# Local attention with q and k kept feature major: rotation halves swapped by DMA, norms applied by GpSimd

## The chip, the cores and the metric

The program runs on one core of one Trainium2 chip. The core has four compute engines that run their own instruction queues in order: TensorE (PE in the profile, its weight loads PEld), VectorE (DVE), ScalarE (ACT) and GpSimd (POOL). SyncE (SP) issues most DMAs; POOL issues some. The metric is device time in microseconds (us) of one execution; less is better.

## The reference, cut to what matters

The whole kernel is four blocks of attention and feed-forward. The change lies in the second stage, `L0_ffn`: two layers of rotary local attention with a gated feed-forward behind it, on 2 sequences of 1024 tokens, which the kernel cuts into 4 blocks of 512 tokens.

```python
qkv = shift_token(x) @ wqkv              # 128 -> 3 * 512
q = l2norm(q) * qs                       # per head of 64: q / sqrt(sum q^2)
k = l2norm(k) * ksc
q = q*cos*scale + rotate_half(q)*sin*scale
k = k*cos/scale + rotate_half(k)*sin/scale
o = local_attention(q, k, v)             # 8 heads, windows of 64 see themselves and the one before
```

`rotate_half` puts the second half of a head's 64 features, negated, before the first. The norm of a token's head is one number, so it can be multiplied in before or after the rotation.

## The kernel before, in words

Class `F0` is this stage. A *unit* is one block of 512 tokens in one layer; there are 8 units (u = 0 to 7; the second layer begins at u = 4). A unit has three parts.

`qkv` (L1593) makes the operands. It transposes x, and then, for each chunk `c` of 128 tokens, multiplies it by the weights three times (q, k, v; `mm3` is three matmuls, L313 to L315, for accuracy), with the tokens on the partitions. For q and k the result is copied by ACT (L1632), squared by ACT (L1635), multiplied on DVE by the sine table in two halves with the halves crossed (L1639) and by the cosine table (L1641), and the squares are summed per head on DVE (L1642). For q the sum of the two products is left to the transposes, which accumulate in PSUM (L1655), and ACT copies the transposed q out (L1656). For k POOL adds the products (L1649). After the four chunks the reciprocal roots are made on DVE (`rsqrt`, L344 to L355); k is multiplied by them on DVE (L1669), transposed and copied out (L1676). The norms of q are left to `score`, which takes them as a scalar.

`scores`/`score` (L1692, L1705, L1707), `turn` (L1717), `shifted` (two POOL DMAs, L1725 and L1726) and `values` (L1736) are the attention, in 8 items per unit, one for each head. `post` (L1746 on) is the output projection, layer norm and feed-forward.

The order of the work is written out by generators. `run` (L1860) goes through the items; `qkv` of unit u+1 (list `A`) is stepped while the items of unit u are issued, `na` = 5 steps for each item, and `posts` (list `B`) `nbt` = 4 steps. A `yield` ends a step. The items of unit u+1 are not issued before its `qkv` is through. The framework then orders each engine's queue by this priority and by when it thinks operands are ready, and sets all the waits. A tile with a `tag` and `bufs=n` has n buffers, and the next user of a buffer waits until all readers of the last are done. `qT`, `kT` and `v` have one buffer for even and one for odd units. `qkv(0)` runs beside the last part of the stage before (its `yield from wait()` takes turns there). `weights_qkv(1)` loads and splits the second layer's weights behind `qkv(3)`; `weights_post(1)` follows `post(3)`.

Of the kernel before, what the change touches and what calls it, by code (L numbers as in the profile page):

```python
# [16 lines left out]
P = 128  # L17
# [1468 lines left out]
def f0_constants():  # L1486
# [13 lines left out]
    rot = out.astype(np.float32).reshape(4, 4, P, 64).transpose(2, 0, 1, 3)  # L1500
# [5 lines left out]
    return {"c_rot": np.ascontiguousarray(rot), "c_band": band, "c_sel8": heads(8)}  # L1506


class F0:
# [3 lines left out]
    wait_rn, wait_h, wait_h7, wait_ta, na, nbt, nta, la, np, ns, npt, pk = 8, 5, 8, 2, 5, 4, 2, 2, 4, 1, 3, 0  # L1513
    banks = dict(s=2, t=2, o=1, b=3)

    def __init__(self, k):
        self.k, self.nc = k, k.nc
        self.w, self.S, self.den = {}, {}, {}
# [12 lines left out]
    def weights_qkv(self, l):  # L1531

        k, nc, d, pool, w = self.k, self.nc, self.k.d, self.more, self.w
        w["qkvh"], w["qkvl"], fill = k.split_w(pool, d["f0_wqkv"][l], 1536, f"wqkv{l}", tag="wqkv")

        tab = k.load(pool, d["c_rot"], [P, 4, 4, 64], f"tab{l}", tag="tab")
        s = [k.bcast(pool, d[nm][l], 64, f"{nm}{l}", tag=nm) for nm in ("f0_qs", "f0_ks")]
        yield from fill
        for j in range(2):
            nc.gpsimd.tensor_tensor(tab[:, 2 * j], tab[:, 2 * j], s[j][:, None, :].to_broadcast([P, 4, 64]), ALU.mult)  # L1540
            for a, b in ((0, 32), (32, 0)):
                nc.gpsimd.tensor_tensor(tab[:, 2 * j + 1, :, a:a + 32], tab[:, 2 * j + 1, :, a:a + 32],
                                        s[j][:, None, b:b + 32].to_broadcast([P, 4, 32]), ALU.mult)
            yield
        w["tab"] = tab

    def weights_post(self, l):
# [15 lines left out]
        raw = k.load(self.more, d["f0_w1"][l], [P, 682], f"w1raw{l}", tag="wraw")  # L1563
# [21 lines left out]
    def operands(self):  # L1585
        k, nc, pool = self.k, self.nc, self.more
        self.xs = [pool.tile([P, T + 1], F32R, name=f"f0x{n}") for n in "hl"]
        for t in self.xs:
            nc.gpsimd.memset(t[64:P, 0:1].bitcast(F32), 0.0)

        self.x0 = [k.dr.tile([P, 4, P], F32, tag=f"f0x0{b}", name=f"f0x0{b}", bufs=1) for b in range(NB)]

    def qkv(self, u, X, tag="t"):  # L1593
# [22 lines left out]
        kr = pool.tile([P, 4, 512], F32, tag="kr", name=f"kr{u}", bufs=1)  # L1616
        ss = pool.tile([P, 2, 4, 8], F32, tag="ss", name=f"ss{u}", bufs=2)
        for _ in range(2):
            yield
        for c in range(4):  # L1620
            cs = slice(c * P, (c + 1) * P)
            for s in range(3):
                yield from wait()
                ps = k.bank("b")
                ws = slice(512 * s, 512 * s + 512)
                k.mm3(ps, xh[:, cs], xl[:, cs], w["qkvh"][:, ws], w["qkvl"][:, ws])
                if s == 2:
                    nc.scalar.copy(v[:, c, :], ps)
                    yield
                    continue  # L1630
                x = kr[:, c, :] if s else pool.tile([P, 512], F32, tag="ta", name=f"ta{u}{c}", bufs=self.nta)
                nc.scalar.copy(x, ps)  # L1632
                yield
                sq = pool.tile([P, 512], F32, tag="sq", name=f"sq{u}{c}{s}", bufs=1)
                nc.scalar.activation(sq, x, AF.Square)  # L1635
                tb = pool.tile([P, 8, 64], F32, tag="tb", name=f"tb{u}{c}{s}", bufs=2)
                x3 = x.rearrange("p (h d) -> p h d", d=64)
                for a, b2 in ((0, 32), (32, 0)):
                    nc.vector.tensor_tensor(tb[:, :, a:a + 32], x3[:, :, b2:b2 + 32],  # L1639
                                            w["tab"][:, 2 * s + 1, c, None, a:a + 32].to_broadcast([P, 8, 32]), ALU.mult)  # L1640
                nc.vector.tensor_tensor(x3, x3, w["tab"][:, 2 * s, c, None, :].to_broadcast([P, 8, 64]), ALU.mult)  # L1641
                nc.vector.tensor_reduce(ss[:, s, c, :], sq.rearrange("p (h d) -> p h d", d=64), AX.X, ALU.add)  # L1642
# [765 lines left out]
```

## Time and profile before

| what | value |
|---|---|
| median of 3 runs (range) | 2244.88 us (2244.24 to 2246.5) |
| profiled execution, its span | 2239.62 us, 2237.9 us |
| PE, DVE, ACT, POOL busy in the span | 91%, 74%, 60%, 22% |
| first score matmul (L1692) of units 0 to 7 | 238.2, 280.7, 322.3, 373.9, 438.7, 482.4, 534.7, 596.4 us |
| last score matmul of unit 7 | 625.4 us |

A *period* is the time from one unit's first score matmul to the next one's. A busy time is the time in which at least one instruction of a group runs. "Releaser" is what ended the idle time before an instruction.

### The profile page before, as it was taken

Reading aid. Unit: us, or ns where it says so; the run is one execution under the profiler, and the core shown is the slowest. Engines: PE = TensorE matmul, PEld = TensorE weight load, DVE = VectorE, ACT = ScalarE, POOL = GpSimd, SP = SyncE. Lnnn points to the kernel's source line nnn. Section 1 sums busy time; section 2 is a strip of 40 time slices with the busy share of each in tenths; the row PEclk is TensorE's granted clock in tenths of the full one; section 3 lists DMA queues with packets and bytes.
Section 4 is the critical chain, followed back from the end, with each engine's and each line's share of the span. In section 5 each row is a group of like instructions: output and inputs, shape, how many; then the busy total and the mean of one; then the engine's idle time right before and its main releaser. Section 6 shows DMA issues by size and latency. Waiting matters only on the chain.

```text
span 2237.9 us, 43122 instructions
## 1 busy us (share of the span) xinstructions
PE 2025.4 (91%) x14400; PEld 1477.7 (66%) x14400; DVE 1664.1 (74%) x5592; ACT 1333.5 (60%) x2983; POOL 501.9 (22%) x706
## 2 busy tenths in 40 slices
PE   7999788888888999999999999998999999999897
PEld 4666566676665667676887665786666566666676
DVE  5778689888878677873777785544777877778787
ACT  3566787787734656665333666333777777767632
POOL 3222212111212532433000322531111111111220
PEclk9999999999978999999999999999999999999999
DMA  5321322021433454421021420604888878888400
GB/s 171 106 77 35 109 50 57 6 48 27 116 113 108 130 175 125 127 65 57 15 67 48 116 78 15 219 17 112 214 209 198 211 192 193 199 194 211 99 5 15
DMA packets 264918, 242.10 MB, mean 108 GB/s; under 512 B 106352, under 2 KB 190618, under 8 KB 263866
## 3 DMA queue, kind: packets, MB, share of 16 engines
q1 hardware_dynamic: 259146, 221.33, 37.2%
q0 software_dynamic: 5232, 17.50, 3.3%
q8 instruction: 115, 1.88, 0.3%
q14 instruction: 105, 0.86, 0.1%
q10 hardware_dynamic: 320, 0.52, 0.1%
HBM read 103.82 MB, written 74.32 MB: 80 GB/s over the span
## 4 chain that ended last, share of the span: by engine, by line
PE 59%; DVE 17%; ACT 10%; DMA 7%; issue 4%; POOL 2%; SPq 1%; ACTq 0%; POOLq 0%; DVEq 0%
PE t L219 5%; PE s L2129 4%; PE o L1393 3%; PE o L744 3%; PE s L695 3%; PE t L728 3%; PE o L1032 3%; PE b L313 3%; PE b L219 3%; PE o L2025 3%; DMA a3dpw<-p 2%; PE s L313 2%; PE b L315 2%; PE b L314 2%; PE s L315 2%
## 5 line engine op out<-in xcount | busy, mean ns | idle before, releaser
L985 DVE CUSTOM_DVE_ANT_0 junk<-w,a1mask 128x640 bf16<-128x640 f32 x256 | 203.1, 818 | 67.3 <-PE w L983 65.4
L219 PE MATMUL t<-ident,p 128*128 128x128 f32 x1280 | 201.9, 279 | 23.8 <-ACT p L1350 15.7
L772 ACT ACTIVATE Pt<-t 128x384 f32<-128x384 f32 (+1 forms) x384 | 179.5, 528 | 65.8 <-PE t L728 54.4
L219 PEld LDWEIGHTS t<-ident,p 128*128 128x128 f32 x1280 | 151.7, 142 | 81.0 <-ACT p L1350 39.0
L1363 ACT COPY PT<-t 128x512 f32<-128x512 f32 x256 | 149.9, 596 | 71.9 <-PE t L219 70.9
L1059 ACT ACTIVATE Pt<-t 128x512 f32<-128x512 f32 x256 | 149.1, 597 | 72.7 <-PE t L1058 44.5
L1350 ACT ACTIVATE p<-s,nb 128x512 f32<-128x512 f32 x256 | 178.6, 702 | 12.8 <-DVE nb L1349 8.4
L1349 DVE TENSOR_REDUCE nb<-s 128x1 f32<-128x512 f32 x256 | 175.0, 687 | 2.6
L1368 DVE CUSTOM_DVE_ANT_0 jk<-p,a3right 128x496 bf16<-128x496 f32 (+3 forms) x256 | 125.0, 488 | 29.2 <-ACT p L1350 17.8
L697 DVE CUSTOM_DVE_ANT_0 junk<-s,a0mask 128x128 bf16<-128x128 f32 (+3 forms) x256 | 114.2, 485 | 43.4 <-PE s L695 42.4
L697 DVE CUSTOM_DVE_ANT_0 junk<-s,a2mask 128x128 bf16<-128x128 f32 (+3 forms) x256 | 114.9, 484 | 28.3 <-PE s L695 27.9
L781 POOL TENSOR_SCALAR_AFFINE_SELECT Pt<-Pt 128x512 f32<-128x512 f32 x112 | 69.9, 636 | 249.0 <-ACT Pt L772 248.9
L1344 PE MATMUL s<-a3KT,a3QT 128*128 128x512 f32 x256 | 118.9, 465 | 7.3 <-DMA a3K<-L 4.1
L1347 DVE TENSOR_TENSOR s<-s,W 128x160 f32<-128x160 f32 (+1 forms) x256 | 81.1, 318 | 56.1 <-PE s L1345 55.2
L1393 PE MATMUL o<-PT,V 128*64 128x512 f32 x512 | 116.9, 599 | 0.5 <-ACT PT L1363 0.5
L1707 ACT ACTIVATE p<-sm,nb 128x128 f32<-128x128 f32 x256 | 100.6, 396 | 24.8 <-DVE nb L1705 24.3
L1345 PE MATMUL s<-a3K,a3Q 128*128 128x512 f32 x256 | 102.7, 401 | 0.1
L1705 DVE CUSTOM_DVE_ANT_0 sm<-s,band,rn 128x128 f32<-128x128 f32 x256 | 78.3, 344 | 26.5 <-PE s L1692 19.3
L1056 PE MATMUL t<-a1Q,a1K 128*128 128x512 f32 (+3 forms) x256 | 92.4, 366 | 6.2 <-ACT Pt L1059 3.6
L695 PE MATMUL s<-a0K,a0Q 128*128 128x256 f32 (+2 forms) x256 | 83.6, 387 | 14.0 <-DVE mx L697 6.8
L982 PE MATMUL w<-a1K,a1Q 128*128 128x256 f32 (+2 forms) x192 | 83.8, 437 | 9.3 <-DVE mx L985 8.3
L2012 ACT ACTIVATE sl<-s 128x512 f32<-128x512 f32 x64 | 38.0, 598 | 91.0 <-PE s L315 85.6
(494 smaller groups left out, 5812.7 us busy)
## 6 DMA issues: line engine op xcount, KB each, us to landing
W<-a3dsk SPq DMA_DIRECT2D x32, 640.0 KB
a1Q<-a1iq SPq DMA_DIRECT2D x32, 512.0 KB
a3dpw<-p SPq DMA_DIRECT2D x64, 160.0 KB
a3dpw<-p SPq DMA_DIRECT2D x64, 144.0 KB
a1K<-a1ik SPq DMA_DIRECT2D x64, 128.0 KB
a3Q<-a3dim SPq DMA_DIRECT2D x32, 256.0 KB
a3KT<-H POOLq DMA_DIRECT2D x64, 128.0 KB, 4.4
a3KT<-H SPq DMA_DIRECT2D x64, 128.0 KB
```

The lines of the kernel that those rows point to most:

```text
L219: return self.nc.tensor.matmul(out.bitcast(x.dtype), x, i[:n, :n], is_transpose=True, start=start, stop=stop)
L695: self.scored = nc.tensor.matmul(s[:, :nm], self.qof(0, t, i)[:, qc * P:(qc + 1) * P], Ks[:, i, :nm], start=True, stop=True).ins
L697: nc.vector.tensor_tensor_reduce(junk[:, :n], s[:, :n], k.mask[:, 512 - n:512], 1.0, NEG, ALU.add, ALU.max, mx[:, qc, i:i + 1])
L772: ready = nc.scalar.activation(Pt[:, i, z:], s[:, z:], AF.Exp, scale=sc).ins
L985: nc.vector.tensor_tensor_reduce(junk, s.rearrange("p a n -> p (a n)")[:, T - n:T + m], k.mask[:, T - n:T + m], 1.0, NEG, ALU.add, ALU.max ...
L1059: nc.scalar.activation(Pt[:, i, :T], s, AF.Exp, scale=sc)
L1344: nc.tensor.matmul(s, QT[:, e, qs], KT[:, e, :], start=True, stop=False)
L1349: nc.vector.tensor_reduce(nb, s, AX.X, ALU.min)
L1350: nc.scalar.activation(p[:, e, :], s, AF.Exp, bias=nb, scale=-1.0, accum_out=den[:, qc, 2 * un + e:2 * un + e + 1])
L1363: self.copied[t] = nc.scalar.copy(PT[e][:, :, qc * P:qc * P + P], tb.rearrange("p (c n) -> p c n", n=P)).ins
L1368: nc.vector.tensor_tensor_reduce(jk[:, :nn], p[:, e, x0:], w["right"][:, :nn], 1.0, 0.0, ALU.mult, ALU.add, at[:, e, qc, 31:32])
L1393: m = nc.tensor.matmul(o[64 * e:64 * e + 64, :], V[:, kc, h * 64:h * 64 + 64], PT[e][:, kc, :], start=(kc == 0), stop=False)
```

## The change

q and k are computed with the features on the partitions: the weights' 128 columns (two heads) are the stationary operand and the 512 tokens stream, so no transposes of q and k follow. For the rotation, a pair of such blocks (`x`, 128 x 2 x 512) is copied by four DMAs on SP into `y` with its groups of 32 partitions exchanged; DVE multiplies `x` by the cosine table into `qT` or `kT`, later `y` by the sine table, and POOL adds the two (`rotate`). The tables are now feature major (1 MB instead of 512 KB) and are scaled on POOL by a column that 12 small DMAs load. The squares (ACT, into the unit's still empty `v`) are summed over each head by a matmul with a 128 x 32 matrix of ones; ACT copies the sums out, POOL's DMAs write them to DRAM, read them back with 128 partitions, DVE makes the reciprocal roots, a POOL DMA writes these to DRAM, and eight POOL DMAs read them back, each row broadcast to 64 partitions. POOL multiplies `qT` and `kT` by them. `score` uses 1.0 instead of the norm. `na` is 6, the extra yields of unit 0 and after `rsqrt` are gone, and the raw `w1` of `weights_post` takes a buffer of the tag `x`, which has two.

```diff
-    wait_rn, wait_h, wait_h7, wait_ta, na, nbt, nta, la, np, ns, npt, pk = 8, 5, 8, 2, 5, 4, 2, 2, 4, 1, 3, 0
+    wait_h7, na, nbt, la, np, ns, npt = 8, 6, 4, 2, 4, 1, 3
...
-        for j in range(2):
-            nc.gpsimd.tensor_tensor(tab[:, 2 * j], tab[:, 2 * j], s[j][:, None, :].to_broadcast([P, 4, 64]), ALU.mult)
...
+        for j in range(4):
+            nc.gpsimd.tensor_scalar(tab[:, j], tab[:, j], sc[:, j:j + 1], None, ALU.mult)
...
-        raw = k.load(self.more, d["f0_w1"][l], [P, 682], f"w1raw{l}", tag="wraw")
+        raw = k.load(self.more, d["f0_w1"][l], [P, 682], f"w1raw{l}", tag="x", bufs=2)
...
+        for s in range(2):
+            dst = (qT, kT[:, :, 64:])[s]
+            for i in range(4):
                 yield from wait()
                 ps = k.bank("b")
+                ws = slice(512 * s + P * i, 512 * s + P * i + P)
+                k.mm3(ps, w["qkvh"][:, ws], w["qkvl"][:, ws], xh[:, 0:T], xl[:, 0:T])
+                if i % 2 == 0:
+                    x = pool.tile([P, 2, T], F32, tag="x", name=f"x{u}{s}{i}", bufs=2)
+                nc.scalar.copy(x[:, i % 2], ps)
+                if i % 2:
+                    y = pool.tile([P, 2, T], F32, tag="y", name=f"y{u}{s}{i}", bufs=2)
+                    for o in (0, 32, 64, 96):
+                        nc.sync.dma_start(y[o:o + 32], x[o ^ 32:(o ^ 32) + 32])
                 yield
+                nc.scalar.activation(v[:, i], x[:, i % 2], AF.Square)
+                nc.vector.tensor_tensor(dst[:, i], x[:, i % 2], w["tab"][:, 2 * s], ALU.mult)
                 yield
+                if i % 2:
+                    for e in range(2):
+                        self.swaps.append((y[:, e], w["tab"][:, 2 * s + 1], dst[:, i - 1 + e]))
+                if len(self.swaps) > 2:
+                    self.rotate()
             yield from wait()
+            ps = k.bank("b")
+            for i in range(4):
+                nc.tensor.matmul(ps[32 * i:32 * i + 32], self.half, v[:, i], start=True, stop=True)
+            yield
+            sr = pool.tile([P, 2, T], F32, tag="x", name=f"sr{u}{s}", bufs=2)
+            nc.scalar.copy(sr[:, 0], ps)
+            for r in range(2):
+                nc.gpsimd.dma_start(rows[8 * s:8 * s + 8].rearrange("(i r) n -> r i n", r=2)[r], sr.rearrange("(i r) a n -> r i a n", r=32)[r, :, 0, :])
+        ss = pool.tile([P, 2, T], F32, tag="x", name=f"ss{u}", bufs=2)[:, 0, 0:64]
+        flat = lambda d: d.rearrange("h (a n) -> (h a) n", n=64)
+        nc.gpsimd.dma_start(ss, flat(rows))
+        for c in range(4):
+            if self.swaps:
+                self.rotate()
...
+            k.mm3(ps, xh[:, cs], xl[:, cs], w["qkvh"][:, 1024:1536], w["qkvl"][:, 1024:1536])
+            nc.scalar.copy(v[:, c, :], ps)
+            yield
+        nc.vector.tensor_scalar(ss, ss, 1e-24, None, ALU.max)
+        y = yield from k.rsqrt(pool, ss, 64, 1)
+        back = k.dr.tile([16, T], F32, tag="f0rn", name=f"f0rn{u}", bufs=2)
+        nc.gpsimd.dma_start(flat(back), y)
+        rn = []
+        for i in range(5):
+            if i < 4:
+                rn.append(pool.tile([P, 2, T], F32, tag="x", name=f"rn{u}{i}", bufs=2))
+                for e in range(2):
+                    src = bass.AP(tensor=back.tensor, offset=back.offset + (8 * (i % 2) + 4 * (i // 2) + e) * T, ap=[[0, 64], [2 * T, 2], [1, T]])
+                    nc.gpsimd.dma_start(rn[i][64 * e:64 * e + 64], src)
+            if i:
+                for e in range(2):
+                    z = (qT, kT[:, :, 64:])[(i - 1) % 2][:, (i - 1) // 2 * 2 + e]
+                    nc.gpsimd.tensor_tensor(z, z, rn[i - 1][:, e], ALU.mult)
+            yield
+        self.S[u] = (qT, kT, v)
+
+    def rotate(self):
+
+        y, tab, dst = self.swaps.pop(0)
+        self.nc.vector.tensor_tensor(y, y, tab, ALU.mult)
+        self.nc.gpsimd.tensor_tensor(dst, dst, y, ALU.add)
```

## The prediction

> **What bounds the stage now.** I read the page first: PE is busy 91% of the whole span, but the change touches only the units between 238.2 and 596.4 us, so I read busy time by windows, one for each period of that stage.
>
> ```profile
> core 0: us, PE busy (x) PEld busy (x) DVE busy (x) ACT busy (x) POOL busy (x), PEclk, DMA share, GB/s
> 238.20:280.70 42.50, 33.95 (x375) 25.96 (x374) 36.20 (x142) 33.37 (x101) 10.97 (x15) 0.92 0.51 138
> 280.70:322.30 41.60, 33.60 (x413) 26.61 (x413) 35.60 (x136) 34.36 (x109) 7.69 (x8) 1.00 0.21 55
> 322.30:373.90 51.60, 45.06 (x462) 35.33 (x463) 45.98 (x152) 40.26 (x111) 12.01 (x15) 0.90 0.16 40
> 373.90:438.70 64.80, 53.82 (x491) 41.37 (x492) 53.04 (x180) 46.35 (x125) 10.25 (x10) 0.90 0.11 29
> 438.70:482.40 43.70, 38.76 (x439) 31.24 (x439) 39.16 (x139) 34.71 (x106) 7.71 (x8) 0.96 0.16 37
> 482.40:534.70 52.30, 44.19 (x475) 35.67 (x475) 45.57 (x165) 40.63 (x113) 7.75 (x8) 0.96 0.12 27
> 534.70:596.40 61.70, 50.02 (x480) 39.00 (x480) 53.75 (x167) 44.08 (x119) 13.64 (x12) 0.93 0.33 94
> ```
>
> The columns are the window, its length, and each engine's busy time. The seven periods sum to 358.2 us and DVE is busy 309.3 of them (86%); the period follows DVE's work (36 us of work in 42, 54 in 62). PE (84%) and ACT (76%) are close behind and POOL idles (20%). Next, the timeline at a unit's start:
>
> ```profile
> 320.90 0.58 ACT L1676 COPY kT<-t 128x512 f32<-128x512 f32 x1 [0.95 <-PE t L219]
> 322.13 0.69 DVE L1669 TENSOR_TENSOR kr<-kr,rn 128x512 f32<-128x512 f32 x1
> 322.28 0.70 PE L1692 MATMUL s<-kT,qT 64*64 64x128 f32 x8 [0.75 <-ACT p L1707]
> ```
>
> A unit's scores start about 1 us after its first kT copy (in every unit: kT at 279.8, 320.9, 372.8, 438.0, 479.6, 534.0, 595.7). So the chain through `qkv` ends last in each period, and DVE's throughput is what paces it.
>
> **DVE.** The groups of the stage, name, shape, count, busy time and mean ns:
>
> ```profile
> L1649 POOL TENSOR_TENSOR kr<-kr,tb 128x512 f32<-128x512 f32 x28 | 35.8, 1278 | 156.2 <-DVE kr L1641 121.4 <-DVE rs L351 8.4 <-DVE rs L344 6.5
> L1641 DVE TENSOR_TENSOR kr<-kr,tab 128x512 f32<-128x512 f32 x28 | 19.2, 684 | 2.0 <-ACT sq L1635 1.9
> ...
> L1639 DVE TENSOR_TENSOR tb<-kr,tab 128x256 f32<-128x256 f32 x56 | 21.7, 422 | 1.6 <-ACT kr L1632 1.4
> ```
>
> Removed per unit: 16 half products (0.42 to 0.49, 7.2 us), 8 products (5.5), 8 sums of squares at 0.678 (5.4), 4 norm products at 0.683 (2.7): 20.8. Added: 8 + 8 products of L1641's shape, 10.9. Net -9.9 us a unit.
>
> **What is given back.** POOL had 5 two-input passes of 1.28 us a unit (4 additions, 1 in `post`); it gets 8 additions and 8 multiplications for the 4 additions, 17 in all. That they disturb DVE shows here:
>
> ```profile
> 344.21 1.29 POOL L1649 TENSOR_TENSOR kr<-kr,tb 128x512 f32<-128x512 f32 x1 [10.11 <-DVE kr L1641]
> ...
> 344.63 1.49 DVE L1639 TENSOR_TENSOR tb<-ta,tab 128x256 f32<-128x256 f32 x2
> ```
>
> The first of those two DVE instructions took 1.15 us instead of 0.42 and ended with POOL's; the same happens three more times to L1639 (1.12 each), to L375 (1.23 for 0.37) and to small `rsqrt` steps (1.18 and 1.21, for about 0.15). Operations that read PSUM beside it (L1705) keep their 0.34. I summed what DVE instructions beside a POOL pass took above the median of their kind: 17.3 us over the stage's 50 passes, 0.35 each. From below it is nothing more per unit; from above each of some 35 DVE instructions with two SBUF operands or of that small kind meets a busy POOL 44% of the time (17 x 1.28 of 50 us) and waits half a pass: 10 us. I take the row's 0.35 x 17 = 6.0 against 17.3 / 8 = 2.2 now: +3.8. DVE then has 6.1 us less a unit.
>
> The Trainium skill says why in SBUF — State Buffer, "Who interferes with whom": a DVE instruction with two SBUF inputs and a GpSimd instruction that reads SBUF share an interface that is locked for a whole instruction. The 1.15 us above agrees. By the rule alone, with random meetings, the loss would be the upper 10 us and DVE would gain nothing.
>
> **ACT and PE.** ACT loses the 8 copies of transposes (0.585) and gets 2 of sums: -3.5 us a unit. PE loses 48 transposes, which the timeline shows 0.11 apart (-5.3), and gets 8 products of 512 columns, two passes each as the other f32 matmuls have, 0.23 apart: +3.7 (0.9 if four column groups ran side by side). Both are beside other work; neither ends a period.
>
> **The new chain.** The sums now cross DRAM twice, on POOL's queue, in order. The nearest rows (size, median us from issue to landing):
>
> ```profile
> f0v<-v POOLq DMA_DIRECT2D x8, 512.0 KB, 5.5
> f0v<-v POOLq DMA_DIRECT2D x8, 384.0 KB, 3.9
> ...
> a3sel<-in_c_sel_dram POOLq DMA_DIRECT2D x1, 256.0 KB, 3.0
> a3right<-in_c_right_dram POOLq DMA_DIRECT2D x1, 128.0 KB, 3.2
> band<-in_c_band_dram POOLq DMA_DIRECT2D x1, 64.0 KB, 3.3
> ```
>
> A small one costs 3.0, an issue 0.54 of POOL. None of these writes DRAM: bounds 1.9 (SP's 8 KB a0Q load, issue at 229.01 to PE at 230.94) and 4.4 (a3KT under load); I take 3.0, the nearest.
>
> When does it start? `v` serves as scratch for the squares, and the buffer is read by unit u-1's values until 10 us after the start of unit u (their last matmuls: 290.6, 332.4, 384.6, against 280.7, 322.3, 373.9). Squares were due at step 4, some 4.5 us; they start at 10.5. Four squares, the half sums and the copy: 15.5. The buffer of tag `x` that the sums hold comes free when they have landed, 19.7; then the last k pair, its squares and sums: copied at 24. From there: the copy 0.6, two row writes 3.6, the read back 3.1, `rsqrt` 4.8 (mean of its eight first-to-last steps, 2.2 to 8.2), the write 3.1, two broadcast reads of 256 KB 4.6, three POOL multiplications 3.9 (both of q, the first of k), and 1.8 for additions still in POOL's queue and for POOL's own waits on DVE: 25.5, with 1 for handing over between engines 26.5. A period can't be under about **50.5 us**, however idle DVE is. Period 1 had no such floor at 41.6.
>
> The remaining multiplications (POOL until about 8 us into the next unit) free the `x` buffers about when the next `qkv` wants them. The waits sit at the head of POOL's queue; behind them stand only additions, `post`'s yb (needed 20 us later) and DMA issues. POOL's own sum is 17 x 1.28 + 16 x 0.54 + 0.3 = 31 us, so it isn't the bound by throughput. The 16 swap DMAs (128 KB each) ride on SP, nearly idle here (DMA share 0.11 to 0.51); the two-deep list of swaps gives them 4 steps, about 4 us: hidden, and 1 to 2 us a unit if not.
>
> **Sum over the periods.** 0: no older values to wait for, 18.6 + 26.5 = 45 (42.5 before). 1, 2 and 4: 50.5 each (41.6, 51.6, 43.7); DVE would allow 45 in period 2, (45.98 - 6.1) / 0.89. 3: today the second layer's weights, behind 39 + 11 steps of 40, delay its first q copy to 24.5 us after the start; with 32 + 11 of 48 steps they fit, but their splits and table passes queue behind POOL's multiplications to 15 or 17: 56 (64.8). 5: `w1raw` holds one of two `x` buffers for some steps, +4: 54.5 (52.3). 6: DVE-paced, (53.75 - 6.1) / 0.87 = 54.8 (61.7). Together 361.8, that is 3.6 more than 358.2. Unit 0's `qkv` lies beside the stage before and today ends at 221.9, 16 us ahead of need; fewer steps pay for its latency, so 0. The profiled execution (span 2237.9, time 2239.62) would take 2243.2; it lies 5.3 under the median of the runs, so the forecast is **2249 us**.
>
> The skill's DMA: Bandwidth & Descriptors, "Anatomy of one DMA — SWDGE (gpsimd) path", fits 2.0 us plus size over 436 GB/s, which is 2.15 for 64 KB; band took 3.3. By the fit the four hops would be about 4 us shorter and the periods about 46.5, the time near 2230.
>
> **The rivals.**
>
> *DVE's relief shows.* If hops land in 1.9 and POOL's queue is empty at each, the floor falls by 4.4 + 1.8 to 44; the periods are then 42, 44.5, 46, 53, 44.5, 49, 54 = 333: **2220**. For it: DVE at 86% is the clear pacer, and 9.9 us leave it. Against: every POOL row is at 3.0 or more.
>
> *GpSimd's chain is slower still.* At 4.4 a hop, 6.4 for the broadcasts and 8.2 for `rsqrt` (its worst, behind other DVE work) the floor is 60: six periods by 6 or more, **2285**. Place: the head of POOL's queue between row write and multiplication. It decides once a hop passes 3.5 us or DVE loses 10 us to POOL. For it: a3KT's 4.4 on the same queue, engines' orders that were set for other latencies.
>
> *The change doesn't act on the bound:* the freed DVE and PE time is already covered; 2245.
>
> **Chances.** Forecast (2238 to 2268) 0.47, relief 0.33, slower chain 0.18, no effect 0.02. A difference under 0.2% (4.5 us) can't be told from none: of the forecast's case 0.03 lies below, 0.14 inside, 0.30 above. So faster 0.36, same 0.16 with the last rival, slower 0.48. Both signs are likely; the forecast's own range is 2238 to 2268, and the whole, from inside the relief to the slow chain, 2212 to 2285.
>
> **What would show it.** Right: periods 1 and 4 near 50 with DVE under 80% busy and POOL above 60%; scores released by POOL's multiplications on kT; DVE products of 1.1 us and more beside POOL's; squares released by values; periods 3 and 6 shorter. Wrong: periods 1 and 4 at or below 44, or scores waiting for something else, above all DVE stuck at the head of its queue on a DMA, or transfers on SP landing late.

## The result, and the profile after

The changed kernel takes 2369.56 us (median of 5 runs, 2364.88 to 2371.88) against 2244.88 us: ratio 1.0556, 95% interval 1.0535 to 1.0577. The forecast was 2249 us with a range up to 2285. The sign was right, but that is little: the forecast lay within 5 us of no change and called both signs likely. The size was off by 120 us. The profiled execution took 2369.56 us too, with a span of 2367.8 us (2237.9 before).

Its units' first score matmuls (now L1708) start at 257.2, 336.5, 400.4, 462.4, 526.0, 587.4, 656.2 and 729.6 us. Unit 0 starts 19.0 us later than before, and the seven periods sum to 472.4 us instead of 358.2. Together that is 133 us; the rest of the program gives 3 back, and the span is 129.9 us longer.

The same view as before, busy time by windows, one for each period (window, length, busy time and instructions of each engine, granted TensorE clock, DMA share, GB/s):

```profile
257.20:336.50 79.30, 40.96 (x398) 26.55 (x397) 32.07 (x126) 34.68 (x106) 29.00 (x37) 0.76 0.47 121
336.50:400.40 63.90, 47.39 (x405) 28.83 (x406) 40.41 (x132) 36.55 (x106) 35.48 (x37) 0.84 0.47 118
400.40:462.40 62.00, 48.50 (x444) 32.53 (x443) 43.97 (x136) 36.66 (x106) 35.96 (x35) 0.89 0.46 116
462.40:526.00 63.60, 46.90 (x411) 29.26 (x410) 39.61 (x132) 36.64 (x106) 39.20 (x39) 0.89 0.37 87
526.00:587.40 61.40, 50.91 (x440) 34.01 (x439) 41.24 (x134) 36.67 (x106) 33.55 (x35) 0.89 0.37 91
587.40:656.20 68.80, 53.70 (x456) 36.54 (x455) 41.55 (x136) 35.11 (x104) 33.52 (x35) 0.88 0.40 97
656.20:729.60 73.40, 49.02 (x424) 32.05 (x423) 56.38 (x163) 41.62 (x113) 37.27 (x39) 0.81 0.54 145
sum 472.40, PE 337.38 PEld 219.78 DVE 295.24 ACT 257.93 POOL 243.98; mean PE 48.20 PEld 31.40 DVE 42.18 ACT 36.85 POOL 34.85
```

No engine is near its limit any more: DVE is busy 295.2 of 472.4 us (62%, 86% before), PE 71%, ACT 55%, POOL 52%. The work hardly shrank (DVE 44.2 to 42.2 us a unit) and the time grew: the engines wait. The timeline of period 1 (336.5 to 400.4) shows for what:

```profile
341.75 1.07 ACT L1635 COPY x<-b 128x512 f32<-128x512 f32 x2 [1.21 <-POOL qT L1685]
...
370.80 0.61 ACT L1655 COPY sr<-b 128x512 f32<-128x512 f32 x1
...
371.70 0.59 POOL L1657 DMA_DIRECT2D f0ss<-sr  x1 [6.48 <-DMA a1iq<-a1c]
...
373.54 0.59 POOL L1657 DMA_DIRECT2D f0ss<-sr  x1
...
377.81 0.59 POOL L1660 DMA_DIRECT2D ss<-f0ss  x1 [2.38 <-DMA f0ss<-sr]
...
380.17 0.82 DVE L1671 TENSOR_SCALAR ss<-ss 128x64 f32<-128x64 f32 x1 [3.15 <-DMA ss<-f0ss]
...
385.31 0.58 POOL L1674 DMA_DIRECT2D f0rn<-rs  x1 [2.39 <-DVE rs L355]
...
387.35 2.36 POOL L1681 DMA_DIRECT2D rn<-f0rn  x4 [0.93 <-DMA f0rn<-rs]
...
392.03 2.53 POOL L1685 TENSOR_TENSOR qT<-qT,rn 128x512 f32<-128x512 f32 x2 [2.31 <-DMA rn<-f0rn]
...
395.07 1.19 POOL L1681 DMA_DIRECT2D rn<-f0rn  x2
...
396.26 2.54 POOL L1685 TENSOR_TENSOR kT<-kT,rn 128x512 f32<-128x512 f32 x2
...
399.54 0.93 PE L1846 MATMUL b<-w,g 128*128 128x128 f32 x6
...
400.40 0.86 PE L1708 MATMUL s<-kT,qT 64*64 64x128 f32 x21
```

A period has three stretches. 5.2 us pass until ACT may copy the first projections, because the buffer of tag `x` is still read by the last unit's multiplications (the releaser in the first line is POOL's L1685). 29 us later the second sums are copied out (370.8); in the same 25 to 30 us most of the attention heads of the running unit are done. Then 29.6 us pass from the second sums to the scores: row writes, read back, `rsqrt`, write, broadcast reads, multiplications, one behind the other. Beside that lie only the last heads (in TensorE's queue until 382) and `post`. In units 1 and 7 TensorE stood idle until POOL's multiplication of kT, where ACT's copy of kT ended the chain before. In period 1 the first of the two multiplications of kT at 396.26 had ended at 397.6, and the scores then stood 2.8 us in TensorE's queue behind matmuls of `post` and of the next projections (the line at 399.54 is the last of these).

The eight norm writes (`f0rn<-rs`) took from 1.8 us, in three units, to 11.8 in unit 1. The DMAs that carry the norms (size, median us from issue to landing; the row writes are 8 KB each):

```profile
rn<-f0rn POOLq DMA_DIRECT2D x64, 256.0 KB, 4.3
...
f0ss<-sr POOLq DMA_DIRECT2D x32, 8.0 KB, 1.8
...
ss<-f0ss POOLq DMA_DIRECT2D x8, 32.0 KB, 2.1
f0rn<-rs POOLq DMA_DIRECT2D x8, 32.0 KB, 3.3
```

### The profile page after: what moved, and what is told of

Read it like the earlier page. It is cut to its first block, busy times and chain, and to the rows that moved or that the text cites. A ratio compares the mean times of both kernels' runs of the same rounds, so it can differ in the third digit from the quotient of the medians.

```text
span 2367.8 us, 43018 instructions
## 1 busy us (share of the span) xinstructions
PE 2064.2 (87%) x14144; PEld 1454.8 (61%) x14144; DVE 1641.6 (69%) x5424; ACT 1307.6 (55%) x2935; POOL 708.5 (30%) x910
## 4 chain that ended last, share of the span: by engine, by line
PE 54%; DVE 15%; DMA 11%; ACT 8%; issue 6%; POOL 4%; SPq 1%; ACTq 0%; POOLq 0%; DVEq 0%
PE s L2145 4%; PE o L1393 3%; PE t L219 3%; PE o L744 3%; PE t L728 3%; PE s L695 3%; PE o L1032 3%; PE o L2041 2%; DMA rn<-f0rn 2%; PE b L313 2%; PE b L219 2%; DVE junk L985 2%; PE s L313 2%; PE s L314 2%; PE s L315 2%
## 5 line engine op out<-in xcount | busy, mean ns | idle before, releaser
L219 PE MATMUL t<-ident,p 128*128 128x128 f32 x1280 | 211.2, 281 | 26.3 <-ACT p L1350 14.8
L219 PEld LDWEIGHTS t<-ident,p 128*128 128x128 f32 x1280 | 152.6, 142 | 102.6 <-ACT p L1350 38.3
L1721 DVE CUSTOM_DVE_ANT_0 sm<-s,band 128x128 f32<-128x128 f32 x256 | 60.9, 284 | 86.6 <-PE s L1708 62.1
L1386 POOL CAST a<-at 128x256 fp32r<-128x256 f32 x32 | 13.1, 410 | 303.6 <-DMA at<-a3dpw 177.5
L982 PE MATMUL w<-a1K,a1Q 128*128 128x256 f32 (+2 forms) x192 | 83.7, 436 | 13.8 <-DVE mx L985 12.3
## 6 DMA issues: line engine op xcount, KB each, us to landing
rn<-f0rn POOLq DMA_DIRECT2D x64, 256.0 KB, 4.3
a3Q<-a3dim SPq DMA_DIRECT2D x32, 256.0 KB
```

The lines of the kernel that those rows point to most:

```text
L219: return self.nc.tensor.matmul(out.bitcast(x.dtype), x, i[:n, :n], is_transpose=True, start=start, stop=stop)
```

## The experiments

The first theory was that the **path through the norms** sets the periods. Its rivals: GpSimd (the lock on DVE, or its throughput), and the new **projection half** itself (swaps, buffers, order). Where a time stands without a ratio, it is one execution; ratios with an interval are against runs of the kernel before on the same chip. Runs of the kernel before lay between 2232.55 and 2253.34 us in these series, so a difference of a few us between single executions says nothing.

**Everything behind the sums left out.**

```diff
-            for r in range(2):
-                nc.gpsimd.dma_start(rows[...], sr...)
-        nc.gpsimd.dma_start(ss, flat(rows))
...
-        y = yield from k.rsqrt(pool, ss, 64, 1)
-        (write, broadcast reads, multiplications)
```

> Leaves out all that follows the sums of squares: the DRAM trips, the reciprocal roots and the multiplications by the norms (the squares, the half-sum matmuls and ACT's copy of the sums stay). Theory T (the period is the serial chain through DRAM on POOL's queue): the 29.6 us from the second copy of sums to the next scores go, and the last addition of k, at about 44 us of the period, is late next: periods 45 to 48 instead of 62, 2230 to 2255 us. Rival L (POOL's passes lock DVE out, throughput): half of POOL's passes go, some 4 us a period, 2330 to 2350. Rival P (the projection half is what is slow: swaps, x buffers, order): under 5 us a period, 2335 or more.

Measured: 2301.5 us, between the theories. Unit 0 starts at 241.7 and periods 0 and 1 are 40.1 and 37.6, shorter than before; but periods 2 to 6 are 57 to 72 us without any norm to wait for. The PE timeline of period 3 (391.0 to 453.9) shows how:

```profile
414.83 1.13 PE L1686 MATMUL s<-kT,qT 64*64 64x128 f32 x16
415.89 0.47 PE L219 MATMUL b<-ident,h 128*128 128x128 f32 x1
...
424.53 0.91 PE L219 MATMUL b<-ident,X 128*128 128x128 f32 x4
```

The next unit's first matmuls (transposes of X) run 33.5 us into the period, behind the last heads and `post`'s transposes of h, in PE's queue, which is in order. With few steps left, `qkv` of unit u+1 is over before `post` begins, and the next one stands behind it: blocks instead of a mixture.

**GpSimd's part.** The norm multiplications on DVE; and, separately, the 14 norm DMAs of a unit on SP's queue.

```diff
-                    nc.gpsimd.tensor_tensor(z, z, rn[i - 1][:, e], ALU.mult)
+                    nc.vector.tensor_tensor(z, z, rn[i - 1][:, e], ALU.mult)
```

> The eight multiplications by the norms on DVE instead of POOL, all else as it is. T: three of them stand between the read and the scores, 0.68 instead of 1.28 each, and the wait moves to DVE's queue: 1 to 3 us less a period, 2345 to 2365. L: half of the passes that lock DVE out are gone: 5 to 10 us less a period, 2300 to 2330.

Measured: 2368.01 us, no difference, and both theories miss, although POOL is busy 9.7 us a unit less and DVE 3.1 more. The way from the second sums to the scores did fall, to 28.3 us in the mean of units 2 to 7 from 29.9, but the seven periods sum to 473.4 us. That GpSimd does the multiplications is not the cause.

```diff
-                nc.gpsimd.dma_start(rows...)   (also ss, back, rn)
+                nc.sync.dma_start(rows...)
```

> The fourteen DMAs of the norms issued by SP instead of POOL. T: each of the four hops is about 1 us shorter (1.9 instead of 3) and POOL no longer stands still at them: 4 to 5 us less a period, 2330 to 2345, if SP is not held by something else; if its queue (swaps, loads of the next stage) holds them, slower than 2369. L: POOL's passes are the same, no change, 2360 to 2375.

Measured: 2370.11 us, no difference: for the time, it doesn't matter which queue issues them.

**No DRAM at all.** Sums token major by 32 small matmuls a unit, q's norm as the scalar of `score`, k's norms transposed and broadcast by PE, DVE multiplies from PSUM.

```diff
-                nc.tensor.matmul(ps[32 * i:32 * i + 32], self.half, v[:, i], ...)
+                    nc.tensor.matmul(ps[:, 8 * c + 2 * i:8 * c + 2 * i + 2], v[:, i, c * P:(c + 1) * P], self.half[:, 0:2], ...)
...
+            nc.tensor.matmul(ps, self.sel[:16, c, :], kn, start=True, stop=True)
+            nc.vector.tensor_tensor(kT[:, c, 64:], kT[:, c, 64:], ps, ALU.mult)
```

> The norms without DRAM and without POOL: the squares are the stationary operand, so the sums come out with tokens on the partitions; q's norms go to the scores as a scalar as before the change, k's are transposed and broadcast by TensorE and multiplied in on DVE from PSUM. T: from the second sums to the next scores about 12 us instead of 29.6, periods near 45: 2225 to 2250. L: eight additions of POOL remain, half the lock: periods near 55, 2300 to 2330. P: 2330 or more.

Measured: 2385.39 us, ratio 1.0653 (1.0615 to 1.0690), slower still. Periods 0 and 1 are 52.2 and 54.8, the others 62 to 79, with PE busy 54.7 us a unit instead of 48.2. The seven sum to 466.0, 6 less than in the changed kernel; what makes this one slower lies behind unit 7's first scores (1657 us to the end instead of 1638), and why is not known. Trading hops for PE's time gained next to nothing in the periods, so DRAM alone is not the fault.

**The swaps left out.**

```diff
-                    for o in (0, 32, 64, 96):
-                        nc.sync.dma_start(y[o:o + 32], x[o ^ 32:(o ^ 32) + 32])
+                        nc.vector.tensor_tensor(y[:, e], x[:, e], w["tab"][:, 2 * s + 1], ALU.mult)
```

> The changed kernel without the 16 swap DMAs of a unit: DVE multiplies x itself by the sine table into y, at once, so the halves are not exchanged and the rotation is not the reference's; everything else, the number of DVE and GpSimd passes too, is as in the changed kernel. S, the swaps matter (the third pair of projections waits until the first pair's x has been read by its swaps, and GpSimd's additions wait for late DVE products): each period falls by 4 to 8 us, 2310 to 2345. R, the path from the sums through the norms sets the end and the swaps run beside it: the squares are read from x, not from y, so the periods fall by under 2 us each, 2355 to 2372.

Measured: 2363.83 us, as R has it: in the time the swaps are hidden, as predicted. Inside the periods the parts move. In the mean of periods 1 to 6 the stretch from the first copies to the second sums is 7 us shorter (22.6, 29.6 with swaps), but the first copies come 4 us later in the period and the way from the sums to the scores is 5 us longer.

**The steps spread**, in the kernel without norms: three steps for each head instead of six.

```diff
-                if s < self.na:
+                if s % 2 == 0 or u == NB - 2:
                     k.step(A)
```

> The kernel without norms (run e1_no_norm: everything behind the sums of squares is left out) with its qkv steps spread out: three of them for each attention head instead of six, so that its 25 steps fill the 8 heads as the 39 of the kernel before did. O, in e1_no_norm the periods 2 to 6 (57 to 71 us) are long because qkv and post stand in blocks behind each other in the order, the transposes of the next unit's x behind all of post: spread out they fall to 50 to 58 each, 2255 to 2280. W, it is the work itself (TensorE busy 84% of these periods at a clock of 0.84 to 0.94): within 10 us of e1_no_norm's 2301.

Measured: 2258.71 us, as O has it: 42.8 us less with not one instruction less. So without norms the feature-major projection needs some 14 us more than the kernel before; the changed kernel, with the norms and the denser steps, needs 111 more. The spread steps were not run with the norms in.

**Buffers of their own for the norms** (on top of the kernel without swaps).

```diff
-                rn.append(pool.tile([P, 2, T], F32, tag="x", name=f"rn{u}{i}", bufs=2))
+                rn.append(pool.tile([P, T], F32, tag="n", name=f"rn{u}{j}", bufs=2))
```

> As e5_no_swap (no swap DMAs, rotation without the exchange), and the norms no longer share the two x buffers: y has one buffer instead of two, and the 4 KB per partition so freed hold the sums read back and the broadcast norms in two half-size buffers of their own (8 reads of 128 x 512 and 8 multiplications as before). B, the next unit's projections are held up until the last unit's multiplications release the x buffers (ACT's first copies of a unit wait for exactly these): they start 5 to 15 us earlier, each period falls by 5 to 12 us, 35 to 80 below e5_no_swap. R, the way from the sums through the norms to the scores alone is what counts, and the next projections could not use the time anyway: within 15 us of e5_no_swap.

Measured: 2424.95 us, 61 more; neither theory. Its reads of 256 KB, each over 128 partitions of one row instead of 64 partitions of two rows, take 8.3 us instead of 4.3, so it tested the buffers badly.

**One trip, or both, in the kernel before.**

```diff
-        nc.vector.tensor_copy(rn.rearrange("p s c h -> p (s c h)"), y)
+        nc.gpsimd.dma_start(back, y)
+        nc.gpsimd.dma_start(rn.rearrange("p s c h -> p (s c h)"), back)
```

> The kernel before, with one part of the change alone: after rsqrt its norms go through DRAM, one GpSimd DMA that writes 128 x 64 numbers and one that reads them back, where a DVE copy was. In the changed kernel such a pair of hops took 4 to 5 us. R, latency on the path from the norms to the scores ends up in the time one to one: 8 units by some 5 us less the copy, 2275 to 2295. H, the kernel before has enough work beside (the next unit's chain has slack): under 10 us, 2240 to 2255.

Measured: 2289.10 us, ratio 1.0199 (1.0179 to 1.0220): R, in the sum. The periods 0 to 6 grow by 12.3, 0.3, 4.8, 8.3, 0.2, 15.3 and 0.9 us, so it isn't shown that each unit pays its own two hops. In period 0 these took 7.3 and 5.6 us, beside the loads of the next stage, elsewhere 1.8 to 3.0 each.

> The kernel before with both trips through DRAM and nothing else of the change: the sums of squares are written and read back by GpSimd DMAs ahead of rsqrt, the norms behind it, four hops a unit as in the changed kernel (there the last one is eight broadcast reads of 128 KB and GpSimd multiplies). One trip alone cost 46 us. R, the trips' latency counts in full: twice that, 2320 to 2345. H, the second trip finds cover: 2285 to 2305.

Measured: 2289.01 us, ratio 1.0202 (1.0166 to 1.0238): H. The second trip, ahead of `rsqrt`, costs nothing on top. So four hops cost 45 us in the old layout; the whole change costs 125.

**More steps early.**

```diff
-    wait_h7, na, nbt, la, np, ns, npt = 8, 6, 4, 2, 4, 1, 3
+    wait_h7, na, nbt, la, np, ns, npt = 8, 12, 4, 2, 4, 1, 3
```

> The changed kernel with one number different: 12 qkv steps for each attention head instead of 6, so that the whole qkv of the next unit stands among the first four heads in the order and the last four heads come behind it. R, a period is the way from a unit's first projection to its scores (58 us, of which 29 are waits for the norms, with the eight heads done in the first 25 to 30 us): with heads left over for the time of the waits, the projections are through earlier and each period falls by 5 to 12 us, 2285 to 2335. O, the order makes it worse: heads that stand behind an instruction that waits for a DMA stop with it, 2370 or more.

Measured: 2384.13 us, ratio 1.0627 (1.0591 to 1.0663): O in the time. But periods 0 to 5 sum to 395.2 us, 4 less than in the changed kernel, and period 6 alone grows, from 73.4 to 91.3. So O's reason, heads behind waits in every unit, is not shown.

**The next stage's constants later.**

```diff
+                if self.nm == "a1":
+                    k.waits(dma.ins, k.mark)     (an earlier score instruction)
```

> The changed kernel; the DMAs that write the next stage's constants (2 MB, on SP, which ran during unit 0's period) wait until units 4 and 5. D, they are why two hops of unit 1's norms took 11.8 and 10.3 us instead of 2 to 5: those hops fall to 5 or less and period 0 from 79 us to 62 to 68, with up to 5 us given back in the periods that the loads move to, 2352 to 2362. N, the hops were slow for another reason: period 0 stays above 74 and the time within 8 us of 2368.

Measured: 2375.70 us. D is right on the cause and not on the gain. POOL's timeline of the changed kernel, first, then of this one, between unit 1's norm write and the first broadcast reads:

```profile
307.98 0.56 POOL L1674 DMA_DIRECT2D f0rn<-rs  x1 [2.38 <-DVE rs L355]
320.10 2.39 POOL L1681 DMA_DIRECT2D rn<-f0rn  x4 [11.55 <-DMA f0rn<-rs]
```

```profile
307.46 0.56 POOL L1678 DMA_DIRECT2D f0rn<-rs  x1 [2.39 <-DVE rs L355]
309.47 2.39 POOL L1685 DMA_DIRECT2D rn<-f0rn  x4 [1.46 <-DMA f0rn<-rs]
```

The write goes from 12.1 to 2.0 us and period 0 from 79.3 to 63.1. But period 5, to which the loads move (SP issues them from 588 to 617 us, and unit 6's swaps stand behind them on SP), grows from 68.8 to 83.2, and period 6 from 73.4 to 79.2.

**Unit 0.** Its steps spaced out as before (two idle steps behind each projection), and its norm work taken off GpSimd:

```diff
+                for _ in range(2 if u == 0 else 0):
+                    yield
```

> The changed kernel with two idle steps behind each of unit 0's eight projections, as the kernel before had: unit 0's qkv then stands more thinly among the work of the stage before. O, unit 0's scores begin 19 us later than before because its qkv was packed more closely into the last part of the stage before and holds up that stage's queues: they begin at 238 to 246 instead of 257, 2350 to 2360. N, the spacing is not the reason: 252 or later, 2362 or more.

Measured: 2365.44 us, unit 0's scores at 256.0: N. In the changed kernel the last multiplication for unit 0 ends at 232.0 and the scores begin at 257.2, so they wait for the stage before and not for the norms.

```diff
-                        nc.gpsimd.dma_start(rn[i]...)         (also rows, ss, back)
+                        (nc.gpsimd if u else nc.sync).dma_start(rn[i]...)
-                        nc.gpsimd.tensor_tensor(z, z, ...)
+                        (nc.gpsimd if u else nc.vector).tensor_tensor(z, z, ...)
```

> The changed kernel with unit 0 alone taken off GpSimd behind its sums: its 14 norm DMAs are issued by SP and its 8 multiplications run on DVE. G, unit 0's scores begin at 257 instead of 238 because waits for DMAs at the head of GpSimd's queue hold up the selects of the stage before: they begin at 240 to 247, 2352 to 2362. N, the stage before is held up by something else (DVE, TensorE's queue): 251 or later, 2363 or more.

Measured: 2363.60 us, scores at 255.75: N. But this doesn't clear GpSimd, for the run trades one hold-up for another. In the changed kernel two small steps of the stage before took 3.47 and 3.85 us on DVE (0.15 to 0.17 alone). The first ended with POOL's multiplications (218.34 and 218.30), the second with the select behind the next two (223.16 and 223.13), and PE waited for the maximum behind each:

```profile
214.87 3.47 DVE L344 TENSOR_SCALAR rs<-lnv 128x4 int32<-128x4 int32 x1
...
215.80 2.50 POOL L1685 TENSOR_TENSOR kT<-kT,rn 128x512 f32<-128x512 f32 x2
...
219.31 3.85 DVE L346 TENSOR_TENSOR rs<-rs 128x4 f32<-128x4 f32 x1
...
220.06 2.49 POOL L1685 TENSOR_TENSOR qT<-qT,rn 128x512 f32<-128x512 f32 x2
...
223.82 0.69 PE L695 MATMUL s<-a0K,a0Q 128*128 128x384 f32 x1 [4.00 <-DVE mx L697]
```

With the norms on SP, the eight broadcast reads stand in SP's queue ahead of a small DMA of the stage before, and PE waits for that one:

```profile
212.97 10.85 SPq L1681 DMA_DIRECT2D rn<-f0rn  x8
223.86 0.57 SPq L568 DMA_DIRECT2D a0Q<-nm  x1
```

```profile
227.41 2.31 PE L728 MATMUL t<-a0Q,a0K 128*128 128x512 f32 x4 [6.84 <-DMA a0Q<-nm]
```

**Broadcasts and multiplications left out**, both trips kept.

```diff
+        rn = pool.tile([P, 2, T], F32, tag="x", ...)[:, 0, 0:64]
+        nc.gpsimd.dma_start(rn, flat(back))
+                for z in (qT[:, 0, 0:64], kT[:, 0, 64:128]):
+                    nc.gpsimd.tensor_tensor(z, z, rn, ALU.mult)
```

> The changed kernel with both trips through DRAM, but the norms are read back once, small (128 x 64), and multiply only 64 columns of the first block of q and of k; the eight broadcast reads and the eight multiplications of 128 x 512 are left out. M, these stand between the norms and the first scores for some 13 us of a unit's 29.6 (read issued at 387.35, scores at 400.40 in period 1) and this counts in full: 8 units by 9 to 11 us, 2275 to 2300. O, with less behind the sums the steps stand in blocks again as in the run without norms (2301): 2300 to 2325. T, the two trips are what costs: 2345 or more.

Measured: 2334.86 us, 35 less, between what O and T say; M needs twice that. Unit 0's scores are back at 238.1: its 19 us go with the broadcasts or the multiplications. The time is 33 us above the kernel without norms and with the same `na` (2301.5). The periods sum to 462.7, only 9.7 less, though the way from the second sums to the scores is 6 to 9 us shorter for units 2 and 4 to 7 (21.5 for unit 4, 29.0 in the changed kernel; unit 3 has 31.3 and 31.2). From period 2 on the next projections begin later by about as much (11.8 us after unit 3's scores, 5.4 in the changed kernel).

**A shorter wait for the first scores.** Each tile holds the norms of one block of q and the same of k.

```diff
-ap=[[0, 64], [2 * T, 2], [1, T]]
+ap=[[0, 64], [8 * T, 2], [1, T]]
```

> The changed kernel with the broadcast norms put together otherwise: each of the four tiles holds the norms of one block of q and of the same block of k, not of two blocks of q or two of k. As many DMAs, bytes and multiplications, but the first scores wait for one read and two multiplications instead of two reads and three. M, latency there counts in full: 4 to 5 us less a unit, 2328 to 2342. N, the later blocks' multiplications then hold up the scores of the next pairs, or the time is set elsewhere: 2358 or more.

Measured: 2375.20 us, ratio 1.0586 (1.0538 to 1.0635): N. The wait is shorter (372.2 to 399.3 in period 1, 27.1 us), but the last of the eight multiplications ends no earlier (38.1 us after the second sums, 36.9 in the changed kernel), and ACT's first copies, which wait for some of them, come 8.0 us after the scores instead of 5.2.

**The sums left out as well** (from the spread kernel without norms).

```diff
-                nc.scalar.activation(v[:, i], x[:, i % 2], AF.Square)
-                nc.tensor.matmul(ps[32 * i:32 * i + 32], self.half, v[:, i], ...)
-            nc.scalar.copy(sr[:, 0], ps)
```

> The kernel without norms and with spread steps (run e7_spread) that leaves out the squares and their sums as well: 8 squares and 2 copies of ACT (6.4 us a unit) and 16 passes of the half-sum matmuls (7 us of TensorE a unit) less. S, they are why e7_spread, with no norms to wait for, is still 15 us slower than the kernel before: 2205 to 2240. N, the projection with its swaps, buffers and order is itself no faster than the old one: 2248 or more.

Measured: 2219.45 us: S. The sums cost 39 us. The busy time over the seven periods, first with the sums and then without:

```profile
sum 370.90, PE 300.77 PEld 207.28 DVE 246.98 ACT 257.66 POOL 120.29; mean PE 42.97 PEld 29.61 DVE 35.28 ACT 36.81 POOL 17.18
```

```profile
sum 332.60, PE 265.39 PEld 202.96 DVE 241.71 ACT 219.30 POOL 117.19; mean PE 37.91 PEld 28.99 DVE 34.53 ACT 31.33 POOL 16.74
```

The periods lose 38.3 us, and PE (35.4) and ACT (38.4) lose as much. That fits a time set by the engines' work here; which engine's is not separated. The bare projection is 25 us faster than the kernel before, which however makes its norms in that time.

**q as in the change, k as before.**

```diff
+                nc.tensor.matmul(ps[:, 8 * c + 2 * i:8 * c + 2 * i + 2], v[:, i, c * P:(c + 1) * P], self.half, ...)
+        nc.vector.tensor_copy(ss[:, 0]..., ps[:, 0:32])
-            for s in range(3):
+            for s in (1, 2):
```

> A whole kernel: q as in the change (feature major, halves swapped by DMA, GpSimd adds), k and v as in the kernel before. The sums of q's squares are made token major, by 16 matmuls with the squares stationary and a 128 x 2 matrix streaming, so that q's norms stay a scalar of score as before and nothing crosses DRAM. By the rows, a unit: DVE 3.4 us less (16 passes for 20), ACT 2.3 less (four copies of transposes), TensorE 32 transposes less (3.5) and 16 small matmuls more (up to 4.6), GpSimd 4 additions more (5.1). G, with no trip on the path the gain shows: 2 to 4 us a unit, 2210 to 2235. N, the small matmuls, GpSimd's additions beside DVE and the swaps on the path to the scores take it back: 2240 or more.

Measured: 2305.66 us, ratio 1.0276 (1.0247 to 1.0304): N. No whole kernel that beats the kernel before was found.

**One x buffer for the norms.**

```diff
+        rn = pool.tile([P, 2, T], F32, tag="x", name=f"rn{u}", bufs=2)
+                nc.gpsimd.dma_start(rn[:, j % 2], src)
+                nc.gpsimd.tensor_tensor(z, z, rn[:, (j - 1) % 2], ALU.mult)
```

> The changed kernel in full, with the broadcast norms in the two halves of one x buffer (one block of 512 tokens each, in the order q, k of a pair of heads; 8 reads of 256 KB and 8 multiplications as before) instead of in both x buffers. The next unit's first pair of projections then doesn't wait for any multiplication (before, ACT's first two copies of a unit waited for them: released at 341.7 and 345.9), and the first scores wait for one block of each. B, the loop over the x buffers paces the units: first copies 3 to 5 us earlier, each period 3 to 6 us shorter, 2325 to 2350. W, the blocks of work that stand behind each other (heads and projections, then post beside the waits) pace them: within 10 us of 2369, though copies and first scores both wait less.

Measured: 2537.70 us, ratio 1.1294 (1.1275 to 1.1313): both theories miss. What PE and ACT waited for between 300 and 700 us, and the reads:

```profile
PE s L1706 <- POOL kT L1682: 58.0, 9, 24.7
...
ACT x L1635 <- POOL kT L1682: 50.8, 4, 15.7
```

```profile
rn<-f0rn POOLq DMA_DIRECT2D x64, 256.0 KB, 7.9
```

The reads are again the form with 128 partitions (7.9 us), they now alternate with the multiplications, and scores of later pairs sit at the head of PE's queue for up to 24.7 us. Whether the `x` buffers pace the periods stays untested.

## Why the prediction was wrong

**The ledger of the runs.** From the kernel before to the bare projection with spread steps, which makes no norms: -25 us (2219). The squares and sums: +39 (2259). The denser order of the steps: +43 (2301). The two trips and `rsqrt`: +33 (2335). The broadcasts and multiplications: +35 (2370), 19 of these at unit 0's start. From the second entry on, each is the difference of two kernels that differ in little but that part, mostly from single executions. Added in another sequence the parts could cost other amounts; above all, it is not shown that the order costs 43 with the norms in.

By the prediction's own steps:

- **What bounds the kernel.** A chain through `qkv` that ends last agrees with the runs: one trip more on it cost 46 us. That it is DVE which paces it was not isolated: the bare projection, 25 us faster, takes work off DVE (44.2 to 34.5 us a unit), ACT (39.1 to 31.3) and PE (42.8 to 37.9) at once.
- **DVE, -9.9 and +3.8 back, -6.1 net.** The busy time fell by only 2.0 a unit (44.2 to 42.2), but this doesn't measure what came back: the windows after hold six `post`s, those before five, and a busy time counts overlapping instructions once. Counted over the seven periods, what DVE instructions (all but L1705, now L1721, which reads PSUM) took beside a POOL pass, above the median of their kind away from one, is 19.0 us before and 49.7 after: 2.7 and 7.1 a unit, 0.39 and 0.40 a pass. So 4.4 came back, and this term was about right. It decided nothing: with the multiplications on DVE the time was the same. The 10 us a unit that the prediction estimated from the rule of the Trainium skill's SBUF — State Buffer, "Who interferes with whom" (the interface is held for whole instructions), were not reached: 7.1.
- **ACT -3.5, PE -1.6.** ACT -2.3. PE +5.4: the term of the half sums was mis-sized. The group of L1652 for units 1 to 7 (name, shape, count, busy us, mean ns):

```profile
L1652 PE MATMUL b<-v,f0half 128*32 128x512 f32 x112 | 51.4, 629 | 1.3 <-ACT x L1635 0.7 <-ACT v L1641 0.3
```

  51.4 us for 7 units are 7.3 a unit, not 3.7, and 0.46 a pass, not 0.23; and the clock fell (0.94 in the mean of the periods to 0.85). The four column groups can run side by side: for unit 0, whose squares were all ready (the last at 163.8), the eight passes for q took 1.04 us, with four starts within 0.02. That would make an estimate of 2.1 a unit. In the periods the squares mostly came one by one, and two passes took as long:

```profile
164.07 1.04 PE L1652 MATMUL b<-v,f0half 128*32 128x512 f32 x8
```

```profile
349.22 1.04 PE L1652 MATMUL b<-v,f0half 128*32 128x512 f32 x2
```

- **3.0 us for each hop.** Medians 1.8 for a row write, 2.1 for the read back and 3.3 for the norm write (1.8 where it was quickest); 4.3 for a broadcast read. The fit of the Trainium skill's DMA: Bandwidth & Descriptors, "Anatomy of one DMA — SWDGE (gpsimd) path", gives estimates of 2.0 to 2.1 for the small hops, nearer for the first two than 3.0, and of 2.6 for a broadcast, too low.
- **26.5 us from the sums to the scores.** Measured 29.6 in period 1. The read back (2.4) and the norm write (2.0) were shorter than priced. But 6.4 passed from the sums' copy to the landed rows (3.6 predicted): POOL put an addition between the two writes, and these took 5.4 and 3.7 us there. And 8.4 passed from the first multiplication to the scores (3.9): POOL issued DMAs for 1.8 between q's and k's, and TensorE had other matmuls in its queue for 2.8.
- **The second sums copied at 24.** This step failed: they came at 34.3, 30.9, 34.6, 31.4, 40.0 and 42.8 us in periods 1 to 6. The squares did not wait for the older values (first one at 6.2, right behind its copy). What came instead: 4 to 12 us until the `x` buffers are free, and then 26 to 35 us for eight projections that share PE, ACT and DVE with the heads. How the second stretch divides between order, buffers and engines was not isolated. With the tail's 3 this makes the six later periods 393.1 us instead of 316.8: 76 of the 126 us that the span missed.
- **Period 0 at 45.** Failed: 79.3. Two hops of unit 1's norms took 12.1 and 11.1 us beside the next stage's loads (148 GB/s, 0.56 of the DMA engines between 300 and 350 us). The loads were there before, in a period of 42.5, and nothing waited for a small DMA beside them. Of the 34 us that were missed here, 16 go with the loads (63.1 with these moved away); the rest is what the later periods lack too.
- **Unit 0's qkv beside the stage before, cost 0.** Failed: 19.0 us. It goes with the broadcasts and multiplications (none of it without them), through what they do to the stage before, for unit 0's own operands were ready at 232.0. The spacing of steps is not the cause. Two hold-ups are seen, DVE beside POOL's multiplications and, with the norms on SP, a small DMA behind the reads; how the 19 us divide stays open. Without the swaps unit 0 began at 248.6, 9 us earlier, so they have a share too.
- **Swaps hidden, POOL's queue harmless.** Right in the time: without the swaps -6, with the DMAs on SP 0.
- **Periods 3 and 6 shorter.** Period 3 by 1.2 only; period 6 is 11.7 longer.
- **The rivals.** The slower chain had the right place, between row write and multiplication, and a third of the size (2285, +40 of 125). That the hops are only part of it, and that the order decides what lies beside them, was in no rival.

The failure common to these: the floor was added up on idle engines. Before the change, as we read it, DVE's work covered a chain through `qkv` of this kind; now little but `post` is left beside 30 us of waits, and heads, projections and waits come one after the other. Shortening the wait for the first scores by 3 us (blocks of q and k together) or 6 to 9 (no broadcasts) then moved the periods by 0 and 1.4 us each: the next unit's first copies came later instead.

## What to carry to other kernels

A serial path of small DMAs is priced by what can still run beside it, not by its hops: sum up the period as blocks that really overlap, and look which buffer the next round needs and when its last reader is done. In-order queues make the written order part of the cost; the same instructions, in the kernel without norms, took 43 us less when they were spread. Look for bulk loads that nothing waited beside: a new small DMA there can take 12 us instead of 2.

## What the runs showed of the hardware

**TensorE's clock follows its idleness.** Between 300.0 and 336.5 us PE is busy 5.9 of 36.5 us, and the granted clock (the third number from the end) is 0.55; the 32 score matmuls behind it take 1.98 us instead of 1.10:

```profile
300.00:336.50 36.50, 5.86 (x41) 4.55 (x41) 6.78 (x14) 1.09 (x2) 11.51 (x15) 0.55 0.58 159
```

```profile
336.53 1.98 PE L1708 MATMUL s<-kT,qT 64*64 64x128 f32 x32 [30.67 <-POOL kT L1685]
```

TensorE: Matmul & The Clock Gate in the Trainium skill, "HAM oscillation — how this bites in real kernels", says that gaps of more than about 3.4 us without matmuls throttle the clock to half; these rows agree. So a long wait on this path is paid twice, the second time in slower matmuls.

**DVE waits for more than one GpSimd pass.** A 128 x 64 step, which takes some 0.2 us alone (L344 behind it: 0.20), beside two back-to-back additions:

```profile
302.47 2.70 DVE L1671 TENSOR_SCALAR ss<-ss 128x64 f32<-128x64 f32 x1
...
302.59 2.52 POOL L1693 TENSOR_TENSOR kT<-kT,y 128x512 f32<-128x512 f32 x2
```

It ends with the second one (305.17 and 305.11): the loss per meeting was counted as half a pass.

**The form of a broadcast read matters.** 256 KB read from DRAM as 64 partitions of two rows took 4.3 us, as 128 partitions of one row 7.9 and 8.3 us in two kernels. In the slower form the outermost dimension of the source's access pattern counts 2 (`[T, 2], [0, 64], [1, T]`), in the faster one 64. The slower kernels had at most two such reads under way and the faster one up to four, so a fuller queue is not the reason; the form was not changed alone.
